# Two layer normalisations in a cross-attention and mixture-of-experts kernel: subtract and multiply replaced by multiply and add

## The chip, the cores and the metric

The kernel runs on one core of one Trainium2 chip. The metric is device time in microseconds (us) of one execution, as the median of several runs. The core has five engines that run side by side and wait for each other by semaphores: TensorE (PE in the profile, with its weight loads as PEld), VectorE (DVE), ScalarE (ACT), GpSimd (POOL) and SyncE (SP, which here only issues transfers).

## The reference

`x` holds 8 batches of 256 channels by 512 positions. Two blocks follow each other, each on a normalised input, each added to its input:

```python
def _layernorm(x, axis=-1, eps=1e-05):
    m = jnp.mean(x, axis=axis, keepdims=True)
    v = jnp.var(x, axis=axis, keepdims=True)
    return (x - m) / jnp.sqrt(v + eps)
...
x = x + _L0_xattn_ref(_layernorm(x, axis=-1), ctx_2048, mask, mask, Wq, bq, Wk, bk, Wv, bv)
x = x + _L0_ffn_ref(_layernorm(x, axis=-1), router_w, shared_gate, shared_up, shared_down, w_gate, w_up, w_down)
```

The first block is cross-attention with 16 heads of 16 channels over 512 by 512 positions; queries come from the normalised `x`, keys and values from the context. The second sees each of the 256 rows of a batch as a token of 512 features: one shared feed-forward network for all, and a router (softmax over 8 experts, the best two) that sends each token to two expert networks of 352 hidden features in bfloat16. The feed-forward block itself returns `x + shared_out + routed` with the normalised tokens as its `x`, so the sum gets the normalised tokens once more.

## The kernel before

The program is one list of instructions in an order written by hand (`tc.manual_schedule()`); each engine takes its own in that order, so an instruction that waits holds up all that stands behind it on its engine. The main loop runs over 8 batches (`b`), 4 groups of heads in each (`g`, in the code `G` counts them over all batches), and 8 steps in each group (`h`); `n = 8 * g + h` numbers the 32 steps of a batch.

In each step TensorE makes two sets of scores: one for the row maximum of a coming group (`row_max`, L453 into the PSUM buffer `s1`, of which there is one), one with the positions turned for the current group (`exp_scores`, L499). VectorE takes the maximum of the first (`nm`, L460), ScalarE the exponential of the second (`e`, L508), and TensorE multiplies it with the values (`attend`, L524). A group ends with `turn_sums` (L539) and `divide` (L554 to L556): the reciprocal of the sums, times the mask (L555), times the summed values (L556). L555 and L556 read two tensors each from the on-chip memory (SBUF).

Between these steps, at step numbers that stand in tables (`ROUTE`, `SHARED`, `FFN`, the conditions on `n`), lie the projections of the next groups (L431, `extra_rows` at L421, L438), the values of the next batch (L393), the shared network of the batch before (L117), its router (`route`, with `hit` at L659, `ranked` at L662, `only` at L668, `left` at L671, `rows` at L710, all small VectorE instructions on two SBUF tensors), and transfers. After the last batch's attention (from about 661 us on) come the expert tiles and the last batch's own feed-forward part.

The change touches the two normalisations. `norm_stats` gives for 128 rows a mean (`mv[:, 0:1]`, VectorE) and an inverse deviation (`rs`, a power on GpSimd at L354).

- The attention normalisation, `start_norm`, runs on GpSimd for batches 1 to 7: steps 9 and 11 of the batch before, one half of the channels each. L374 makes `xm` from `x`; L375 multiplies it by the mask `mb`. Between or before them stand the two L361 of `mask_context` (context times mask, step 8, in batch 0 step 10). Batch 0's own normalisation is written out elsewhere (`shifted`, `scaled`, L1211).
- The token normalisation, `token_norm`, runs once for each half of a batch's tokens: on GpSimd for batches 0 to 6, on VectorE for the last batch. L575 makes `xn`; L576 adds it to the running sum `acc`; on GpSimd the cast to bfloat16 (L604) and a memset (L605) follow for the first half, and TensorE turns `xn` (L594).

Of the kernel before, what the change touches and what calls it, by code (L numbers as in the profile page):

```python
# [9 lines left out]
F32 = mybir.dt.float32  # L10
# [3 lines left out]
ALU = mybir.AluOpType  # L14
# [3 lines left out]
P = 128  # L18
# [22 lines left out]
def xattn_ffn_kernel(  # L41
# [20 lines left out]
    nc = tc.nc  # L62
# [3 lines left out]
    def pool(name, bufs, **kw):  # L66
        return ctx.enter_context(tc.tile_pool(name=name, bufs=bufs, **kw))
# [6 lines left out]
    four = pool("four", 4)  # L74
# [280 lines left out]
        return mv, rs  # L355


    def mask_context(b, engine=nc.gpsimd):
        s = S[b]
        for i in range(2):  # L360
            engine.tensor_mul(s["ctx"][:, i, :], s["ctx"][:, i, :], s["mb"])  # L361
# [5 lines left out]
    def start_norm(b, i):  # L367

        s = S[b]
        if i == 0:  # L370
            s["xm"] = one.tile([P, 2, T], F32, tag="xm", name=f"xm{b}")
        xm = s["xm"]
        mv, rs = s["stats", i]
        nc.gpsimd.tensor_scalar(xm[:, i, :], s["x"][:, i, :], mv[:, 0:1], rs, ALU.subtract, ALU.mult)  # L374
        nc.gpsimd.tensor_mul(xm[:, i, :], xm[:, i, :], s["mb"])  # L375

    def project_v(b, sc):
# [192 lines left out]
    def token_norm(b, tt, engine=nc.gpsimd):  # L570
        s = S[b]
        acc = s["acc", tt]
        mv, rs = s.pop(("tstats", tt))
        xn = one.tile([P, T], F32, tag="rd", name="xn")
        engine.tensor_scalar(xn, acc, mv[:, 0:1], rs, ALU.subtract, ALU.mult)  # L575
        engine.tensor_add(acc, acc, xn)  # L576
        s["xn", tt] = xn

# [631 lines left out]
    busy(6)  # L1210
    nc.vector.tensor_scalar(s0["xm"][:, 1, :], s0["xm"][:, 1, :], s0["stats", 1][1], None, ALU.mult)  # L1211
    mask_context(0, nc.vector)
    q_part, q_rows = project_qk(0, 0)
    k_part, k_rows = project_qk(0, 1)
# [27 lines left out]
    for i in range(3):  # L1242
# [11 lines left out]
        out=mwide, in_=mask.rearrange("b o (n t) -> (b o n) t", t=32).rearrange("p (o t) -> p o t", o=1).to_broadcast([P, 4, 32])  # L1254
# [32 lines left out]
    def clear(i):  # L1287
# [8 lines left out]
    clears = [(1.0, lambda i=i: clear(i)) for i in range(E * PIECES)]  # L1296
    FFN = {
        0: {4: residual, 6: token_stats, 7: token_norm, 9: turn_tokens, 14: round_tokens},
        2: {6: residual, 7: token_stats, 8: token_norm, 9: turn_tokens, 10: round_tokens},
    }  # L1300
    LAST_FFN = {3: residual, 5: token_stats}
# [55 lines left out]
    for b in range(B):  # L1357
# [13 lines left out]
        if 0 < b < B - 1:  # L1371
            spread(plan, route(b - 1), ROUTE)
            units, early = shared_units(b - 1, True)
            spread(plan, units, SHARED)
            plan[28].append(early)
        elif b == B - 1:
            units, early = shared_units(b - 1, True)
            spread(plan, units[:24], SOONER)
            plan[20].append(early)
            units = units[24:]  # L1380
            first_rows = route(b - 1, rows_first=True)
            row_map, expert_numbers = expert_map(0)
            fetch, named, experts, tiles = expert_tiles()
            spread(plan, first_rows, FIRST_ROWS)
            spread(plan, row_map, ROW_MAP)
            plan[FETCH_AT] += expert_numbers + [fetch]
            plan[22] += [lambda: ring.remove(0)]
            plan[22] += [go for _, go in units[:2]]
            units = units[2:]
            plan[29] += [lambda: divide(last - 2), lambda: experts(0)]  # L1390
            plan[26] += [lambda: token_norm(b, 0, nc.vector)]
        later = plan[STEPS:]
        plan = plan[:STEPS]
        for g in range(NG):
            G = NG * b + g
            for h in range(8):
# [44 lines left out]
                if b + 1 < B:  # L1441
                    if n == (4 if b else 8):
                        load_batch(b + 1)
                    elif n == 7 and b:
                        start_stats(b + 1, 0)
                    elif n == (8 if b else 10):
                        mask_context(b + 1)
                    elif n == 9 or n == 11:
                        start_norm(b + 1, n // 11)
                    elif n in V_AT:  # L1450
                        for sc, kc in V_AT[n]:
                            if kc == 0:
                                NEWV[sc] = project_v(b + 1, sc)
                            if kc < 2:
                                NEWV[sc][0](kc)
                            else:
                                NEWV.pop(sc)[1]()
# [109 lines left out]
```

## Time and profile before

| | |
|---|---|
| median of 3 runs | 799.71 us (797.23 to 801.35) |
| the profiled execution | 799.23 us, of which the span from first to last instruction is 797.5 |
| busy, share of the span | TensorE 96%, VectorE 71%, ScalarE 43%, GpSimd 41% |
| L374, 14 on GpSimd | 2111 ns each |
| L575, 14 on GpSimd and 2 on VectorE | 2090 ns and 546 ns each |

A row of the time line reads: start in us from the span's start, duration in us, engine, line of the program, operation, the tiles it writes and reads (`out<-in`), shapes, number of instructions in the row, and in brackets how long the engine idled before it and what ended that. A row of the groups has in place of the times, behind the bar, the busy time in us of all of them, the mean of one in ns, and the idle time before them. The chain that ended last is followed back from the last instruction, at each step to what released it; its shares say which engine set the end.

### The profile page before, as it was taken

The page shows a single profiled execution, that of the slowest core. Times are in us where ns is not written, and L with a number is a line of the kernel's source. Part 1 is how long each engine was busy: PE and PEld are TensorE (multiplying, and loading weights), DVE is VectorE, ACT ScalarE, POOL GpSimd, SP SyncE. Part 2 cuts the span into 40 slices and gives each one's busy share as a digit, 9 for nine tenths or more (in the row PEclk, how much of TensorE's full clock was granted, in tenths as well). Part 3 has the DMA queues.
Part 4 walks back from the last instruction along what each step waited for, and adds up shares of the span by engine and source line. Part 5 has one row for each costly group of instructions (what it writes and reads, how often), then busy time and mean ns, then how long its engine had stood idle before and what let it go on. Part 6 is the DMA issues. An engine that isn't in the chain of part 4 may idle for free.

```text
span 797.5 us, 14542 instructions
## 1 busy us (share of the span) xinstructions
PE 764.1 (96%) x5317; PEld 315.2 (40%) x5317; DVE 566.8 (71%) x1088; ACT 346.4 (43%) x428; POOL 324.8 (41%) x451
## 2 busy tenths in 40 slices
PE   8987897999999999999999999999999999999996
PEld 5322231343333333343334333433343343665672
DVE  7676767678777877787778777888687767563315
ACT  4234444444444444443444444444444445455640
POOL 4006132804193319331843174317550234376530
PEclk9999999999999999999999999999999999999999
DMA  5115669721255325532454132210000001596739
GB/s 177 37 52 174 223 210 260 188 46 20 72 102 91 81 59 105 99 83 59 100 103 83 42 65 67 65 41 28 30 1 1 28 30 37 120 188 149 149 121 351
DMA packets 102208, 78.49 MB, mean 98 GB/s; under 512 B 69512, under 2 KB 87858, under 8 KB 101754
## 3 DMA queue, kind: packets, MB, share of 16 engines
q1 hardware_dynamic: 93674, 56.29, 26.8%
q0 software_dynamic: 5136, 20.46, 11.5%
q10 hardware_dynamic: 3328, 0.81, 0.6%
q8 instruction: 43, 0.70, 0.4%
q14 instruction: 27, 0.22, 0.1%
HBM read 38.09 MB, written 43.38 MB: 102 GB/s over the span
## 4 chain that ended last, share of the span: by engine, by line
PE 86%; DVE 11%; issue 1%; DMA 1%; ACT 0%; POOL 0%; ACTq 0%; DVEq 0%; POOLq 0%
PE s L453 33%; PE av L524 13%; DVE nm L460 8%; PE psy L117 4%; PE psk L431 4%; PE psq L431 4%; PE pg L117 4%; PE psv L117 3%; PE pu L117 3%; PE ey L947 3%; PE pgu L117 3%; PE s L499 3%; PE eg L927 3%; PE eu L927 3%; PE pht L939 1%
## 5 line engine op out<-in xcount | busy, mean ns | idle before, releaser
L508 ACT ACTIVATE e<-s 128x1024 f32<-128x1024 f32 x256 | 261.7, 1024 | 347.1 <-PE s L499 335.9
L460 DVE TENSOR_REDUCE nm<-s 128x2 f32<-128x1024 f32 x248 | 304.0, 1226 | 139.8 <-PE s L499 123.7
L453 PE MATMUL s<-k,q 32*128 32x512 f32 x1024 | 288.5, 641 | 19.1 <-DVE nm L460 17.2
L499 PE MATMUL s<-q,k 32*128 32x512 f32 x1024 | 285.5, 640 | 1.9 <-DMA q<-nmt 0.9
L524 PE MATMUL av<-e,V 128*32 128x512 f32 x1024 | 136.5, 604 | 0.0
L453 PEld LDWEIGHTS s<-k,q 32*128 32x128 f32 x1024 | 76.9, 183 | 125.0 <-DVE nm L460 115.2
L564 POOL TENSOR_TENSOR acc<-acc,x 128x512 f32<-128x512 f32 x15 | 19.0, 1268 | 186.0 <-DVE acc L563 150.3
L499 PEld LDWEIGHTS s<-q,k 32*128 32x128 f32 x1024 | 77.0, 183 | 7.4 <-ACT e L508 5.0
L354 POOL TENSOR_TENSOR rs<-ve,mhalf 128x1 f32<-128x1 f32 x32 | 18.5, 578 | 136.6 <-DVE ve L352 136.6
L421 POOL TENSOR_SCALAR extra<-mb,alpha,beta 128x512 f32<-128x512 f32 x60 | 45.9, 773 | 48.9 <-DVE q L438 22.8
L524 PEld LDWEIGHTS av<-e,V 128*32 128x32 f32 x1024 | 20.4, 108 | 97.2 <-issue 73.1
L117 PE MATMUL psy<-sdT,h 128*32 128x256 f32 (+2 forms) x336 | 54.3, 393 | 0.5 <-DVE h L1041 0.5
L933 DVE SCALAR_TENSOR_TENSOR hz<-eth,eu 128x352 bf16<-128x352 f32 x39 | 20.3, 520 | 35.1 <-PE eu L927 18.3
L209 POOL DMA_INDIRECT xs<-xnb,at x32 | 34.6, 1080 | 21.8 <-DVE at L718 11.3
L117 PEld LDWEIGHTS psy<-sdT,h 128*32 128x32 f32 (+1 forms) x336 | 29.4, 140 | 33.9 <-issue 30.6
L117 PE MATMUL pg<-xT,sguT 128*32 128x256 f32 (+1 forms) x284 | 37.0, 380 | 0.0
L117 PE MATMUL pu<-xT,sguT 128*32 128x256 f32 (+1 forms) x284 | 36.8, 382 | 0.0
L117 PE MATMUL psv<-WvT,ctx 128*128 128x256 f32 (+1 forms) x170 | 36.5, 401 | 0.0
L431 PE MATMUL psq<-xm,WqT 128*128 128x512 f32 x64 | 35.6, 641 | 0.5 <-DVE xm L1211 0.5
L117 PE MATMUL pgu<-xT,sguT 128*32 128x256 f32 (+2 forms) x234 | 35.7, 382 | 0.0
L431 PE MATMUL psk<-ctx,WkT 128*128 128x512 f32 x64 | 35.4, 640 | 0.0
L927 PEld LDWEIGHTS <-late_ctx 128*128 128x128 bf16 x312 | 29.2, 98 | 13.8 <-issue 1.3
(210 smaller groups left out, 883.4 us busy)
## 6 DMA issues: line engine op xcount, KB each, us to landing
xs<-blank SPq DMA_DIRECT2D x32, 544.0 KB
x<-in_x_dram SPq DMA_DIRECT2D x7, 512.0 KB
ctx<-in_ctx_dram SPq DMA_DIRECT2D x7, 512.0 KB
accd<-acc SPq DMA_DIRECT2D x12, 256.0 KB
again<-accd POOLq DMA_DIRECT2D x12, 256.0 KB, 3.9
out_dram<-again SPq DMA_DIRECT2D x12, 256.0 KB
gu<-in_L_ffn_w_gate_dram POOLq DMA_DIRECT2D x8, 352.0 KB, 6.2
gu<-in_L_ffn_w_up_dram POOLq DMA_DIRECT2D x8, 352.0 KB, 4.5
```

What stands on the lines that cost most here:

```text
L117: nc.tensor.matmul(ps[cols], weights[:, cols], moving, **flags)
L209: i = nc.gpsimd.indirect_dma_start(to[:, :], bass.IndirectOffsetOnAxis(ap=rows, axis=0), what, None, **bounds).ins
L421: engine.tensor_scalar(t, S[b]["mb"], at, be, ALU.mult, ALU.add)
L431: nc.tensor.matmul(ps, W[:, kc, g // 2], rhs[:, kc, :], start=(kc == 0), stop=(kc == 1),)
L453: nc.tensor.matmul(ps[:, jj, :], q[r, tci * P : (tci + 1) * P], k[r, :], start=True, stop=True)
L460: best = lambda: nc.vector.reduce_max(to, ps, axis=AX.X)
L499: nc.tensor.matmul(ps[:, jj, :], k[r, sc * P : (sc + 1) * P], q[r, :], start=True, stop=True)
L508: nc.scalar.activation(e, ps, AF.Exp)
L524: nc.tensor.matmul(AVT[G][32 * j : 32 * j + 32, :], V[:, sc, g // 2, j, g % 2 : g % 2 + 2, :].rearrange("p o d -> p (o d)"), et[j // 2][:, ...
L927: nc.tensor.matmul(ps, xT[:, kc, :], weights_of(t, GU, I, (m * NKC + kc) * I), start=(kc == 0), stop=(kc == NKC - 1),)
L933: nc.vector.scalar_tensor_tensor(HZ[t % 2], th, 1.0, pu, ALU.add, ALU.mult)
L947: nc.tensor.matmul(ps, ht[:, ic, :], weights_of(t, DN, T, ic * T), start=(ic == 0), stop=(ic == 2))
```

## The change

A new function, `normal`, makes a column `off = mean * rs * (-1)` and then `out = row * rs + off`. Both normalisations call it, on the engine they ran on before. The column is one more instruction on one element per partition, on GpSimd 28 times and on VectorE twice; the large instruction stays one, with the same shapes and two column operands, and its operations are a multiply and an add instead of a subtract and a multiply. The large instruction waits for the column by a semaphore on its own engine. `off` has four buffers. On all other engines the order of instructions stays as it was.

```diff
+    def normal(out, row, stats, engine):
+
+        mv, rs = stats
+        off = four.tile([P, 1], F32, tag="off", name="off")
+        engine.tensor_scalar(off, mv[:, 0:1], rs, -1.0, ALU.mult, ALU.mult)
+        engine.tensor_scalar(out, row, rs, off, ALU.mult, ALU.add)
+
...
         xm = s["xm"]
-        mv, rs = s["stats", i]
-        nc.gpsimd.tensor_scalar(xm[:, i, :], s["x"][:, i, :], mv[:, 0:1], rs, ALU.subtract, ALU.mult)
+        normal(xm[:, i, :], s["x"][:, i, :], s["stats", i], nc.gpsimd)
         nc.gpsimd.tensor_mul(xm[:, i, :], xm[:, i, :], s["mb"])
...
     def token_norm(b, tt, engine=nc.gpsimd):
         s = S[b]
         acc = s["acc", tt]
-        mv, rs = s.pop(("tstats", tt))
         xn = one.tile([P, T], F32, tag="rd", name="xn")
-        engine.tensor_scalar(xn, acc, mv[:, 0:1], rs, ALU.subtract, ALU.mult)
+        normal(xn, acc, s.pop(("tstats", tt)), engine)
         engine.tensor_add(acc, acc, xn)
```

## The prediction

> **What bounds the kernel now.** I read the page from the top: engines and the chain that ended last, then the GpSimd groups, then the time line of VectorE and GpSimd wherever the distance between two row maxima (`nm`, L460) was longer than usual.
>
> ```profile
> PE 764.1 (96%) x5317; PEld 315.2 (40%) x5317; DVE 566.8 (71%) x1088; ACT 346.4 (43%) x428; POOL 324.8 (41%) x451
> PE 86%; DVE 11%; issue 1%; DMA 1%; ACT 0%; POOL 0%; ACTq 0%; DVEq 0%; POOLq 0%
> ```
>
> TensorE is busy 96% of the span and GpSimd (POOL), which the change relieves, is 0% of the chain. From 60 to 661 us the kernel beats in steps of 2.45 to 2.60 us: TensorE makes scores in one PSUM buffer, VectorE takes their maximum in 1.23 us, and the next scores go 0.09 us later into the same buffer. In a batch of 32 steps TensorE idles under 1 us of 81. So a VectorE instruction that ends late in its step moves everything behind it; a GpSimd instruction matters only through VectorE.
>
> ```profile
> L421 POOL TENSOR_SCALAR extra<-mb,alpha,beta 128x512 f32<-128x512 f32 x60 | 45.9, 773 | 48.9 <-DVE q L438 22.8 <-DVE share L685 15.4 <-DVE k L438 10.2
> L374 POOL TENSOR_SCALAR xm<-x,mv,rs 128x512 f32<-128x512 f32 x14 | 29.6, 2111 | 0.0
> L575 POOL TENSOR_SCALAR xn<-acc,mv,rs 128x512 f32<-128x512 f32 x14 | 29.3, 2090 | 1.2
> L726 POOL TENSOR_SCALAR xnb<-place 128x1 int32<-128x1 f32 x32 | 7.2, 226 | 4.5 <-DMA xs<-xnb,at 2.5
> ```
>
> Behind the bar of each row stand the busy time in us, the mean of one instruction in ns, and the idle time before them. L421 is a multiply and an add with two column operands, which is what the normalisations become; L374 and L575 are a subtract and a multiply of the same shape. Next, how the engines touch each other (VectorE first, then GpSimd, the sixth of the seven attention normalisations):
>
> ```profile
> 471.35 0.17 DVE L555 TENSOR_TENSOR rd<-rd,mturn 128x16 f32<-128x16 f32 x1
> 471.55 1.38 DVE L556 TENSOR_TENSOR O<-u,rd 128x256 f32<-128x256 f32 x1
> 473.01 1.21 DVE L460 TENSOR_REDUCE nm<-s 128x2 f32<-128x1024 f32 x1
> ...
> 469.18 2.08 POOL L374 TENSOR_SCALAR xm<-x,mv,rs 128x512 f32<-128x512 f32 x1
> 471.34 1.31 POOL L375 TENSOR_TENSOR xm<-xm,mb 128x512 f32<-128x512 f32 x1
> ```
>
> L556 usually takes 0.42 us. Here it ends 0.28 us after L375 does: a VectorE instruction that reads two SBUF tensors waited for GpSimd. The step took 3.08 us instead of 2.50. Of all VectorE instructions only eight are stretched this way, by 4.5 us in all, and three of the steps are longer for it: at 62.23 us (L555 and L556 behind both L361; 4.04 us), at 469.93 and at 551.61 (3.08 each). That is 1.6 + 0.6 + 0.6 us, the most that the change could give back here.
>
> **GpSimd's own gain.** The small operation is not in the trace. One column costs 0.19 us as a copy (L727), 0.226 as one add (L726), 0.578 as a power (L354). L421's own fixed part is its 0.773 less what 511 more columns cost a cast (L604 0.622 against L727 0.187): 0.34. I take 0.28, between L726 and that; 0.20 and 0.58 stay as ends. A GpSimd instruction that waits for the one before starts 0.09 us later (L374 to L375: 471.26 to 471.34). So a normalisation takes 0.28 + 0.09 + 0.77 = 1.14 us instead of 2.09: 0.95 us less, 27 us over 28. TensorE waits for L575 in 2 places and 1.2 us in all, so none of the 27 is on the path: GpSimd waits longer for VectorE instead. What counts is that what follows each normalisation on GpSimd comes 0.95 us (behind two, 1.9 us) earlier, and which two-input VectorE instruction it then meets.
>
> **Token normalisation, six batches (starts 180.50, 261.69, 343.15, 424.69, 506.40, 588.07).** In each, L659 starts 1.23 us after L575:
>
> ```profile
> 181.73 0.17 DVE L659 TENSOR_TENSOR hit<-w,best 128x16 f32<-128x16 f32 x1
> 181.93 0.17 DVE L662 TENSOR_TENSOR hit<-hit,rank 128x16 f32<-128x16 f32 x1
> 182.67 1.23 DVE L460 TENSOR_REDUCE nm<-s 128x2 f32<-128x1024 f32 x1 [0.57 <-PE s L499]
> ...
> 180.50 2.08 POOL L575 TENSOR_SCALAR xn<-acc,mv,rs 128x512 f32<-128x512 f32 x1
> 182.66 1.28 POOL L576 TENSOR_TENSOR acc<-acc,xn 128x512 f32<-128x512 f32 x1
> ```
>
> Both lie under L575's second half and are not held. After the change: column 180.50 to 180.78, `xn` 180.87 to 181.64, L576 (two inputs, 1.27 us) ready at 181.73, just when L659 starts. At 471.34 and 471.35 such a tie went to VectorE. Then L576 runs 181.90 to 183.17, and L662, due at 181.93, ends near 183.20. The maximum, due at 182.67, starts at 183.12: 0.45 us late. 0.08 us of that is slack (it ends 0.17 us before the next scores, where 0.09 is enough). 0.37 x 6 = +2.2 us.
>
> **Attention normalisation, seven batches.** First (60.17): L375 ends at 62.67 instead of 63.62, the two L361 at 65.15 instead of 66.06, and L556 behind them 0.9 us sooner: -0.9, all on the path. Second: L375 runs 143.74 to 145.01 and holds L555 (144.86) for 0.15 us, which idle time covers. Third to fifth: the second normalisation is ready at 227.36, L556 starts at 227.34: VectorE first, 0; if GpSimd is 0.1 us earlier, L556 waits until 228.13 and the maximum is 0.4 us late: 0 to +1.2 for three. Sixth and seventh: L375 now runs 469.44 to 470.72, the second normalisation 471.09 to 471.86 holds L555 until 471.88, and L556 (471.92) ties with the second L375 (471.95). VectorE first: 0.58 better than before; GpSimd first: 0.58 worse. I take 0, bounds -1.2 to +1.2. A late L421 in the last batch meets L556 near 594.5: +0.1.
>
> [...]
>
> **The two on VectorE (672.58 and 692.7).** Each gets one more column instruction; the nearest row is L352, 0.154 us, plus 0.03 before the next. The first stands in a stretch (661 to 674) with no idle VectorE, ahead of L576 and L556: +0.2. The second has idle time around it: 0. The large instruction stays at its 0.546 us. Ends 0 and +0.4. Nothing moves on TensorE, ScalarE or SyncE; the casts and scatters on GpSimd's queue start up to 1 us earlier and nothing waits for them there.
>
> **Sum.** -0.9 + 2.2 + 0 + 0.1 + 0.2 = +1.6 us. The profiled execution took 799.23 (span 797.5 and 1.7 around it): 800.8. It lies 0.48 under the median of 799.71, so 801.3.
>
> **Rivals.** *The column is cheap, and GpSimd wins the ties (slower).* With 0.20 us L576 is ready at 181.65, 0.08 ahead of L659, as the second L361 (64.80) was ahead of L556 (64.91) and won. L659 then waits until 182.95; the cast L604 (0.62 us), which follows L576 without a gap, takes its turn before L662 as the second L361 did; L662 ends near 183.5 and the maximum is 0.78 late, 0.70 beyond slack: x 6 = 4.2. The third to fifth batch lose their 1.2. 4.2 + 1.2 - 0.9 + 0.3 = +4.8: 804.5. It decides below about 0.23 us for the column. For it: L726's 0.226. Against: two operands and two operations, as L421's fixed 0.34.
>
> *The column is dear (faster).* At L354's 0.58 us `xn` ends at 181.94; L659 and L662 pass before L576, covered by 0.57 us of idle time. The first batch gains 0.6, sixth and seventh 0.5 each, less 0.3 at the end: -1.3, so 798.4. The same comes about if 16-element instructions slip through; L555 at 63.72 took 1.16 and speaks against that.
>
> *The change does not do what it says:* the new form takes 2.09 us, and the column is added. Then GpSimd is 0.37 us later each time: the sixth and seventh batch's L556 escape L375 (-1.0), the first gains 0.8, +0.3 at the end: -1.5, 798.2. Sixty L421 at 0.773 speak against it.
>
> **Chances.** Forecast 0.42, cheap column 0.37, dear column 0.12, no effect on the form 0.09. 0.5% is 4.0 us, about what a measurement of this kernel can tell from no change (its three runs span 4.1). Slower: 0.31 of the cheap column, 0.06 of the forecast with the ties against it, 0.01 else: 0.38. Faster: 0.06, from the last two with the ties for them. Same: 0.56. The range reaches from under the last two, 797.5, to above the cheap column, 805.5.
>
> **What would show it.** Right: the normalisations on GpSimd near 0.77 us, the column near 0.28; L662 near 1.2 us in six batches with steps near 2.95; the step at 62 us near 3.2. The cheap column: L659 near 1.2 too, steps over 3.2. Wrong altogether: L659 and L662 at 0.17 and still a change beyond 4 us; or TensorE waiting on something other than the row maximum.

## The result, and the profile after

The changed kernel takes 797.51 us (median of 12 runs, 796.05 to 798.31) against 799.78 for the kernel before (12 runs, 797.23 to 802.85). The ratio is 0.9956, with a 95% interval of 0.9941 to 0.9971: some 2.3 to 4.7 us faster, where 1.6 us slower was forecast. That the median lies at the very lower end of the forecast's range (797.5) is luck: this end came from two rivals, a dear column and a form without effect, and neither of them happened. The profiled execution took 796.99 us, 795.2 of it the span.

The page of the changed kernel, engines and chain (its line numbers are 5 to 7 higher behind the new function: L453 is L459, L499 L505, L375 L381, L576 L581, L662 L667):

```profile
PE 762.2 (96%) x5317; PEld 315.2 (40%) x5317; DVE 573.4 (72%) x1090; ACT 346.4 (44%) x428; POOL 295.0 (37%) x479
PE 85%; DVE 12%; issue 1%; DMA 1%; ACT 0%; DVEq 0%; ACTq 0%
```

GpSimd lost 29.8 us of work, VectorE gained 6.6 us of occupied time, and the chain is TensorE and VectorE as before. The groups of the changed kernel on GpSimd (and, last, the column on VectorE):

```profile
L363 POOL TENSOR_SCALAR xm<-x,rs,off 128x512 f32<-128x512 f32 x14 | 11.6, 825 | 1.4
L363 POOL TENSOR_SCALAR xn<-acc,rs,off 128x512 f32<-128x512 f32 x14 | 10.7, 767 | 1.4
L362 POOL TENSOR_SCALAR off<-mv,rs 128x1 f32<-128x1 f32 x28 | 7.5, 267 | 1.2
...
L362 DVE TENSOR_SCALAR off<-mv,rs 128x1 f32<-128x1 f32 x2 | 0.4, 192 | 0.7 <-POOL rs L354 0.7
```

The prices were right: 0.767 us for the large instruction (0.825 in the attention, where some waited for VectorE), 0.267 for the column. So were most of the places named. The forecast new wait is there, in the time line of VectorE and GpSimd in the third batch:

```profile
260.69 0.16 DVE L664 TENSOR_TENSOR hit<-w,best 128x16 f32<-128x16 f32 x1
260.89 1.12 DVE L667 TENSOR_TENSOR hit<-hit,rank 128x16 f32<-128x16 f32 x1
261.94 1.21 DVE L466 TENSOR_REDUCE nm<-s 128x2 f32<-128x1024 f32 x1
...
259.82 0.77 POOL L363 TENSOR_SCALAR xn<-acc,rs,off 128x512 f32<-128x512 f32 x1
260.67 1.30 POOL L581 TENSOR_TENSOR acc<-acc,xn 128x512 f32<-128x512 f32 x1
```

L581 starts 0.02 us before L664, and yet L664 is not held (0.16 us). L667 is: it ends 0.04 us after L581, after 1.12 us instead of 0.17. The step is 2.91 us long instead of 2.60.

To see where time went I took the time from each row maximum to the next in two traces and listed the steps that differ. A second trace of before (e1, below) is the base, since single traces have stretches in which, by their clock record, TensorE was granted half its clock: the first trace of before has one from 32.4 to 35.8 us (mean granted clock 0.51, 1.1 us lost), the one of the changed kernel none until its end.

| place in the trace of the changed kernel | step before to after | change, next step included |
|---|---|---|
| 61 us, L561 free of the first L368 | 4.04 to 3.08 | -0.96 |
| 157 us, scores L505 hardly late (0.25 us) | 3.48 to 2.73 | -0.75 |
| 177 us, L664 and L667 wait | 2.60 to 3.39 | +0.66 |
| 259, 340, 422, 503, 585 us, L667 waits | 2.60 to 2.91 | +0.18 each |
| 470 and 551 us, L562 free of L381 | 3.08 to 2.50 | -0.50 each |
| all steps from 54 to 659 us | | -1.1 |

The first row on VectorE, in the first trace of before and then after: the second of the two instructions is still held, the first no longer.

```profile
63.72 1.16 DVE L555 TENSOR_TENSOR rd<-rd,mturn 128x16 f32<-128x16 f32 x1
64.91 1.44 DVE L556 TENSOR_TENSOR O<-u,rd 128x256 f32<-128x256 f32 x1
```

```profile
62.73 0.19 DVE L561 TENSOR_TENSOR rd<-rd,mturn 128x16 f32<-128x16 f32 x1
62.95 1.44 DVE L562 TENSOR_TENSOR O<-u,rd 128x256 f32<-128x256 f32 x1
```

The second row was in no term of the forecast. TensorE around it, with two weight casts of GpSimd and four small transfers of SyncE ahead of it, in the first trace of before and then after:

```profile
151.79 0.61 POOL L333 DMA_DIRECT2D d<-in_L_ffn_w_down_dram  x1
152.51 2.45 SPq L481 DMA_DIRECT2D q<-nmt  x4
153.04 0.49 POOL L333 DMA_DIRECT2D gu<-in_L_ffn_w_gate_dram  x1
...
157.41 1.13 PE L453 MATMUL s<-k,q 32*128 32x512 f32 x4
158.61 1.13 PE L499 MATMUL s<-q,k 32*128 32x512 f32 x4
```

```profile
147.02 0.60 POOL L333 DMA_DIRECT2D d<-in_L_ffn_w_down_dram  x1
148.24 0.49 POOL L333 DMA_DIRECT2D gu<-in_L_ffn_w_gate_dram  x1
150.56 3.97 SPq L487 DMA_DIRECT2D q<-nmt  x4
...
155.46 0.70 PE L459 MATMUL s<-k,q 32*128 32x512 f32 x2
155.71 0.70 PE L505 MATMUL s<-q,k 32*128 32x512 f32 x2
```

At the first scores of a later group the two kinds run side by side: in the fourth batch of the changed kernel L459 starts at 318.82 us and L505 at 318.94. Here, before, L499 starts 1.2 us after L453: the first scores of a new group wait for `q`, into which four small transfers write the row maxima (`take_max`, L481, `q<-nmt`). The casts moved from 0.7 us before and 0.5 us behind the first of these transfers to 3.5 and 2.3 us before it.

### The profile page after: what moved, and what is told of

Same layout as the page of the kernel before. It is cut to its first block, busy times and chain, and to the rows that moved or that the text cites. A ratio compares the mean times of both kernels' runs of the same rounds, so it can differ in the third digit from the quotient of the medians.

```text
span 795.2 us, 14572 instructions
## 1 busy us (share of the span) xinstructions
PE 762.2 (96%) x5317; PEld 315.2 (40%) x5317; DVE 573.4 (72%) x1090; ACT 346.4 (44%) x428; POOL 295.0 (37%) x479
## 4 chain that ended last, share of the span: by engine, by line
PE 85%; DVE 12%; issue 1%; DMA 1%; ACT 0%; DVEq 0%; ACTq 0%
PE s L459 32%; PE av L530 13%; DVE nm L466 9%; PE psy L117 4%; PE psq L437 4%; PE psk L437 4%; PE pgu L117 4%; PE pg L117 4%; PE ey L952 3%; PE psv L117 3%; PE eg L932 3%; PE eu L932 3%; PE s L505 3%; PE pu L117 2%; PE pht L944 1%
## 5 line engine op out<-in xcount | busy, mean ns | idle before, releaser
L459 PE MATMUL s<-k,q 32*128 32x512 f32 x1024 | 287.8, 639 | 19.0 <-DVE nm L466 16.5
L505 PE MATMUL s<-q,k 32*128 32x512 f32 x1024 | 285.0, 639 | 1.8 <-DMA q<-nmt 0.8
L459 PEld LDWEIGHTS s<-k,q 32*128 32x128 f32 x1024 | 76.7, 183 | 124.8 <-DVE nm L466 115.9
L505 PEld LDWEIGHTS s<-q,k 32*128 32x128 f32 x1024 | 76.8, 183 | 6.2 <-ACT e L514 4.9
```

The costliest lines, as they stand in the source:

```text
L459: nc.tensor.matmul(ps[:, jj, :], q[r, tci * P : (tci + 1) * P], k[r, :], start=True, stop=True)
L505: nc.tensor.matmul(ps[:, jj, :], k[r, sc * P : (sc + 1) * P], q[r, :], start=True, stop=True)
```

## The experiments

Theory A (in the expectations the VectorE or place theory): the gain is what VectorE waits less for GpSimd, plus chance. Theory B (the transfer theory): besides, GpSimd's queue, 2 to 3 us ahead after several shorter normalisations, starts its weight casts (L333, 352 KB each) earlier, and the small transfers into `q` are no longer slowed by them. Theory C (the clock theory): the change raises the granted clock.

Each kernel ran in 8 to 12 runs beside 19 to 35 of before on the same chip. Because the times go with the mean granted clock (before, beside e5: 799.45 us at 0.997, 806.31 at 0.99), the table also gives the time at a granted clock of 0.998, from a straight line fitted with one slope to all runs that were taken together (0.58 to 0.65 us per 0.001; standard error of a value 0.25 to 0.4 us).

| run | ratio to before (95%) | at equal clock, against before |
|---|---|---|
| e1 before again | 1.0002 (0.9980 to 1.0024) | 800.4, 800.0 |
| e2 attention only | 0.9948 (0.9928 to 0.9967) | 798.0, 800.0 |
| e3 token only | 1.0002 (0.9982 to 1.0022) | 800.3, 800.0 |
| e4 before, cast early | 0.9987 (0.9966 to 1.0009) | 799.6, 800.0 |
| e5 after again | 0.9966 (0.9949 to 0.9982) | 798.6, 799.8 |
| e6 after, pause | 0.9963 (0.9945 to 0.9982) | 796.7, 799.8 |
| e7 after, cast late | 1.0007 (0.9993 to 1.0021) | 801.5, 799.8 |
| e8 after, old work too | 1.0019 (0.9999 to 1.0039) | 802.0, 799.8 |
| e9 after, two pauses | 0.9935 (0.9908 to 0.9961) | 796.1, 800.0 |
| e10 after, third time | 0.9957 (0.9938 to 0.9975) | 798.2, 800.0 |
| e11 = e6 again | 0.9957 (0.9941 to 0.9973) | 795.7, 798.4 |
| e12 = e8 again | 1.0014 (0.9993 to 1.0034) | 800.4, 798.4 |

**e1, before again** (no edit).

> The kernel before, unchanged, for a second trace. Two theories of where the gain came from. VectorE theory: only what GpSimd holds VectorE up for has changed (L555 and L556 at about 62, 472 and 553 us; new waits of L662 in six batches), and the rest of the difference between the two traces (a stretch at half clock from 32.4 to 35.8 us in the one of before, late scores L499 at about 158, 321 and 403 us) is chance: then these last are not there again in this trace, and the steps at 62, 470 and 552 us are long as before (4.04, 3.08, 3.08). Transfer theory: the late scores at about 158, 321 and 403 us belong to the kernel before, because its casts L333 start just ahead of the small transfers from nmt into q; then L499 is late by 0.35 to 1.2 us there again. Time: same as before within 0.2% by both.

The steps at 61 (4.04), 468 and 550 us (3.08) came back to the hundredth, and so did the late scores in the second batch (L499 0.99 us late, step 3.48). Those near 321 and 403 us did not. So the first belongs to the kernel, the other two come and go.

**e2, the attention normalisation alone; e3, the token normalisation alone.**

```diff
 e2: start_norm calls normal(...); token_norm keeps
+        engine.tensor_scalar(xn, acc, mv[:, 0:1], rs, ALU.subtract, ALU.mult)
 e3: token_norm calls normal(...); start_norm keeps
+        nc.gpsimd.tensor_scalar(xm[:, i, :], s["x"][:, i, :], mv[:, 0:1], rs, ALU.subtract, ALU.mult)
```

> Only the attention normalisation (L374) is a multiply and an add; the token normalisation is as before. VectorE theory: -0.96 at 62 us, -0.5 each at 472 and 553 us, no new wait of L662: about 2.0 us faster than before, so 0.3 to 1 us faster than the whole change. Transfer theory adds what the earlier casts bring: GpSimd's queue is 2 us ahead after two normalisations instead of 3 to 4, the casts L333 lie 1 to 2 us further from the small transfers, and the late scores at 158, 321 and 403 us shrink or vanish: 2 to 3.5 us faster than before.

> Only the token normalisation (L575) is a multiply and an add. VectorE theory: L662 waits in six batches (+0.18 to +0.37 each), the step at 62 us stays at 4.04, and the chain on GpSimd ahead of L375 is 1 us earlier in six batches, so that L375 lies from 470.4 to 471.7 and L555 waits for it a little: time within 0.15% of before, by -1 to +1.5 us. Transfer theory: the casts come 1 us earlier, and the late scores at 158, 321 and 403 us are there but shorter: -1.5 to +1.

The attention half holds all of the gain. In e2 the steps at 64, 470 and 552 us shrink by 0.95, 0.5 and 0.5, scores are at most 0.25 us late, nothing waits in the router; but in the second to fifth batch a new wait of 0.2 to 0.4 us appears (steps of 2.83 to 2.96), because with one shorter normalisation instead of two GpSimd meets the divide in another place. e3 has its six new waits (+0.18 each), late scores still at 162 and 325 us (0.5 us each, as theory B expects of casts that come only 1 us earlier), the same new waits at the divide, and yet the steps at 470 and 552 us are short as well: one shift of 1 us is enough to take L381's counterpart away from the divide. Its time is that of before. All this was expected in kind, but e3's gain at 470 and e2's new waits had not been seen ahead.

**e4, before with the cast of step 11 at step 7.**

```diff
-                plan[5 * n + 1].append(casts.pop(0))
+                plan[(1, 6, 7, 16, 21, 26)[n]].append(casts.pop(0))
```

> The kernel before with one edit: in batches 1 to 4 the cast that stood at step 11 (L333, d<-w_down) stands at step 7, ahead of the attention normalisation in GpSimd's queue. The normalisations are as before. VectorE theory: nothing that GpSimd holds VectorE up for changes, the time is that of before. Transfer theory: the transfers from nmt into q (step 13) no longer share the DMA engines with that cast, the late scores at 321 and 403 us go, and at 158 us, where two casts stood around, half of it: 0.6 to 1.6 us faster than before.

The step near 161 us went from 3.48 to 3.03, half, as theory B has it for one of two casts. In the later batches e1 had no late scores that could go. The time, 0.13% less, cannot be told from none; the fall that theory B expected was 0.6 to 1.6 us.

**e5, after again.**

> The changed kernel again, beside runs of before on the same chip. The first four runs showed two parts: steps that differ in the traces (about -1.0 us for the whole change against a second trace of before, counted place by place), and stretches at half clock, of 3.4 us each, which come at different places in each run and cost some 0.6 us per 0.001 of mean granted clock. Place theory: the change is worth 1 to 2 us, and what the medians show beyond that is chance of the clock; then the mean granted clock of its runs is that of the runs of before within 0.001. Clock theory: less work on GpSimd lets the clock be granted more often; then its mean clock is again over that of before by 0.002 or more, and the time lower by 2.5 to 4 us. In the trace both expect no late scores L505 after 60 us, the long steps at about 177 (3.39) and four or five of 2.91.

The same steps as in the first trace, place by place; the count gives -1.3 us against e1, and at equal clock it is 1.2 us faster than before. Its mean granted clock is 0.0023 over that of before, which is what the clock theory expected.

**e7, after with that cast one step later; e8 and e12, after with the old work added.**

```diff
 e7
-                plan[5 * n + 1].append(casts.pop(0))
+                plan[(1, 6, 12, 16, 21, 26)[n]].append(casts.pop(0))
 e8, e12, in start_norm behind the mask multiply
+        mv, rs = s["stats", i]
+        nc.gpsimd.tensor_scalar(spare, s["x"][:, i, :], mv[:, 0:1], rs, ALU.subtract, ALU.mult)
```

> The changed kernel with the cast of step 11 (L333, d<-w_down, batches 1 to 4) at step 12, behind one scatter in GpSimd's queue, so that in batches 2 to 4 it starts about 1 us before the small transfers from nmt into q, as in the kernel before. Transfer theory: late scores come back in batches 2 to 4 (0.2 to 0.5 us each, at about 238, 319, 400 us), not in batch 1, where the queue has no scatter at that place: +0.3 to +1.2 us over the changed kernel. If the late scores have another cause: no late scores and the same time.

> The changed kernel, and behind each mask multiply of the attention normalisation GpSimd also does the old subtract and multiply (2.1 us, 14 times) into a tile that nobody reads (bfloat16, for room). GpSimd is as busy as before and its queue is 2 us later after each half. Clock theory: the mean granted clock falls to that of before (about 0.993 to 0.995). Place theory: the clock stays with that of the changed kernel; only places move: the casts L333 start later again, so the step near 157 us is long again (3.0 to 3.6 instead of 2.73), and L562 at 62 us escapes one of the two context multiplies: within 1.5 us of the changed kernel.

At equal clock e7 is 3.0 us slower than the changed kernel and 1.8 slower than before, by the start of three casts. Theory B had the places right and the size wrong (0.3 to 1.2 us). GpSimd, SyncE and TensorE of e7 in the fourth batch:

```profile
317.77 0.58 POOL L333 DMA_DIRECT2D d<-in_L_ffn_w_down_dram  x1
...
318.53 3.35 SPq L487 DMA_DIRECT2D q<-nmt  x4
...
323.43 1.13 PE L459 MATMUL s<-k,q 32*128 32x512 f32 x4
325.12 1.13 PE L505 MATMUL s<-q,k 32*128 32x512 f32 x4 [0.56 <-ACT logT L1061]
```

The cast starts 0.76 us ahead of the four transfers. Issuing them takes 3.35 us instead of 2.2, and L505 is 1.69 us late (the step takes 4.18 us). The profile puts the wait down to ScalarE's `logT`, which L505 does not read and which in the changed kernel's own trace runs after L505 has begun (`logT` from 319.79 to 320.16 us, L505 from 318.94); what L505 does read is `q`. The transfer records of the traces show it. For the 64 packets of 128 bytes that such a group of four moves, the table gives when the last packet ends and when the last semaphore of the four reports its landing, both counted from the start of the first issue:

| kernel, batch | cast starts before the transfers by | last packet after | landed after | scores late by |
|---|---|---|---|---|
| all, no cast near | | 2.96 to 3.22 us | up to 3.6 us | mostly 0.12 us |
| after, third to fifth | 3.6 us | 3.00 to 3.02 | 3.57 to 3.63 | 0.12 |
| after, second (two casts) | 3.5 and 2.3 | 4.71 | 5.01 | 0.25 |
| before, third | 1.0 | 3.66 | 3.98 | 0.12 |
| e1, third to fifth | 1.0 | 3.64 to 3.94 | 4.06 to 4.62 | 0.15 to 0.20 |
| before, fourth and fifth | 1.0 | 4.27, 4.26 | 5.10, 5.23 | 0.40, 0.46 |
| before, second (two casts) | 0.7, and 0.5 behind | 5.20 | 5.96 | 1.19 |
| e7, third | 0.7 | 6.03 | 6.86 | 2.09 |
| e7, fourth and fifth | 0.8 | 4.99, 4.56 | 6.39, 5.33 | 1.69, 0.56 |

The scores are due 4.9 us after the first issue. Where the landing came within 4.62 us they were at most 0.26 us late (before, after, e1); where it came after 5.01 us or more, they started 0.13 to 0.20 us behind it, in every trace. So the landing is what they wait for. In the changed kernel's second batch the transfers are still slowed (last packet after 4.71 us), but land after 5.01 us, 0.1 behind the due time. Where the transfers lose the time is not separated: issuing them takes longer too, up to 3.97 us instead of 2.24. Part of it is in the packets. In the second batch of before, 16 packets of a cast (22.5 KB and about 2 us each) start from 153.10 to 153.71 us, and the first of them to end does so at 155.46; the first small packet, which with no cast near starts 1.2 us after the first issue (175.15 against 173.98), starts 3.0 us after it, at 155.51. That fits the shared DMA engines of e4's expectation; the records name a packet's queue, not its engine.

e8 shows the same from the other side: with GpSimd as far behind as before, its casts start 0.1 us before to 0.3 us behind the transfers, and four batches have late scores (0.7 to 2.3 us). At equal clock it is 3.5 us slower than the changed kernel, where the place theory expected at most 1.5. That two causes, the extra work and the lateness, are in e8 together is why e7 is the cleaner case: it has the same work as the changed kernel.

**e6 and e11, after with a pause before the add.**

```diff
         normal(xn, acc, s.pop(("tstats", tt)), engine)
+        if tt == 0 and 0 < b < B - 1:
+            engine.memset(pause, 0.0)
         engine.tensor_add(acc, acc, xn)
```

> The changed kernel with one more instruction: in batches 1 to 6 a memset of 128 x 512 bfloat16 (write only, about 0.5 us) on GpSimd between the first token normalisation and the add that follows it, so that L664 and L667 pass before the add reads SBUF. If those waits cost what the place count says (0.66 at 177 us, 0.18 in each of five batches, 1.5 us in all), the six long steps go back to about 2.6, L667 to 0.17 us, and the time is 1.0 to 1.6 us under the changed kernel's, unless the clock differs. If they are hidden: same time as the changed kernel.

GpSimd now writes for 0.53 us, without reading a tensor, while the two router instructions pass. VectorE, then GpSimd, of e6:

```profile
259.65 0.17 DVE L667 TENSOR_TENSOR hit<-w,best 128x16 f32<-128x16 f32 x1
259.85 0.17 DVE L670 TENSOR_TENSOR hit<-hit,rank 128x16 f32<-128x16 f32 x1
260.59 1.23 DVE L467 TENSOR_REDUCE nm<-s 128x2 f32<-128x1024 f32 x1 [0.57 <-PE s L506]
...
258.79 0.77 POOL L364 TENSOR_SCALAR xn<-acc,rs,off 128x512 f32<-128x512 f32 x1
259.49 0.53 POOL L583 MEMSET pause<- 128x512 bf16 x1
259.99 1.26 POOL L584 TENSOR_TENSOR acc<-acc,xn 128x512 f32<-128x512 f32 x1
```

All six long steps are gone, and the count against e1 is -3.0 us where e5 has -1.3. The medians of e5 and e6 do not show it (799.31 and 799.36), since e6's runs happened to have a clock 0.0024 lower; at equal clock e6 is 1.9 us under e5.

**e9, e6 and a second pause; e10, after beside it.**

```diff
                     elif n == (8 if b else 10):
+                        for _ in range(0 if b else 4):
+                            nc.gpsimd.memset(pause, 0.0)
                         mask_context(b + 1)
```

> The changed kernel with the pause before the add of the token normalisation (as in e6) and four such write-only memsets (about 2.1 us) on GpSimd ahead of the two context multiplies L368 in batch 0, so that the divide of that time (two SBUF inputs) passes before them. By the place count the step at 61 us goes from 3.1 to about 2.5 (-0.6) on top of the 1.5 us of e6: 2.1 us under the changed kernel, 3 us under before at the same clock. If it is hidden or only moves: the step at 61 us or the next one is longer by the same 0.6.

> The changed kernel once more beside e9 on the same chip, to compare the two there: e9 is 1 to 2.5 us faster than this, with their mean granted clocks taken into account. Its own mean clock against that of before says again whether the clock goes with the change (0.002 or more above) or with chance.

The step at 62 us is 2.45, as long as its neighbours, where the first trace of before had 4.04. e9 is the fastest kernel here, ratio 0.9935 against 0.9957 for the changed kernel beside it, 2.1 us at equal clock.

**e11 and e12, for the clock.**

> The kernel of e6 again, for the clock. So far the kernels without the old attention form (e2, e5, e7, e9, e10) had a mean granted clock 0.0015 to 0.0034 over that of before in the same call, those with it (e1, e3, e4, e8) -0.0003 to +0.0005, and e6, without it, -0.0001. If the old form's work on GpSimd is what costs clock, this run comes out 0.0015 or more above before, and the time at 0.995 of it; if the clock is chance, anything from -0.002 to +0.003.

> The kernel of e8 again, in which GpSimd also does the old subtract and multiply, for the clock. If that work costs clock: its mean clock is within 0.0008 of that of before and 0.0015 or more below e11's. If the clock is chance: no such order. The late scores near 158, 241, 324 and 409 us come back by the transfer theory, and the time is 2 us or more above the changed kernel's.

The mean granted clock against before was +0.0023 and +0.0034 for the changed kernel (e5, e10), +0.0022 for e2, but -0.0001 and +0.0015 for one and the same kernel (e6, e11), and +0.0006 and +0.0018 for the other (e8, e12), +0.0015 for e7, +0.0021 for e9 and within 0.0004 of it for e1, e3 and e4, mostly with a standard error near 0.0008. That the old form's work costs clock is not borne out: e12 has that work and the higher clock. Theory B held in e12: late scores in the same four batches, and at equal clock 2.0 us slower than before.

## Why the prediction was wrong, point by point

- **GpSimd's own gain: right.** Column 0.28, measured 0.267; form 0.77, measured 0.767; none of it on the path directly.
- **Token normalisation, +2.2 forecast, +1.6 measured.** Mechanism and place were right in five of the six batches; a wait there costs 0.18 and not 0.37, because the step is 0.31 longer and the next gives 0.13 back. At 177 us GpSimd won the tie (L581 at 178.79, L664 at 178.83), and it cost 0.66, close to the 0.70 that the cheap column rival gave; in e5 and e12 it went the same way, in e7, e8 and e10 VectorE won, so it is a matter of hundredths (GpSimd 0.04 us ahead here, 0.02 us ahead at 260.67, where L664 was not held).
- **First attention normalisation, -0.9 forecast, -0.96 measured;** third to fifth 0 and 0 (L562 went first and the normalisation was the one stretched, to 1.01 to 1.05 us). The late L421 forecast near 594.5 (+0.1) did not show.
- **Sixth and seventh: 0 taken, -0.5 each measured.** The tie went to VectorE as at 471.35 in the trace of before. VectorE first, then GpSimd, in the changed kernel:

```profile
469.01 0.48 DVE L561 TENSOR_TENSOR rd<-rd,mturn 128x16 f32<-128x16 f32 x1
469.53 0.43 DVE L562 TENSOR_TENSOR O<-u,rd 128x256 f32<-128x256 f32 x1
...
468.71 0.77 POOL L363 TENSOR_SCALAR xm<-x,rs,off 128x512 f32<-128x512 f32 x1
469.56 1.52 POOL L381 TENSOR_TENSOR xm<-xm,mb 128x512 f32<-128x512 f32 x1
```

  L561 waits for the second normalisation, L562 follows 0.03 us before L381, and L381 is the one that is stretched (1.52 instead of 1.27). The same reasoning that was used for the token ties would have given VectorE here; taking the middle cost 1.0 us.
- **The step that failed: "the casts and scatters on GpSimd's queue start up to 1 us earlier and nothing waits for them there".** They start 2.6 to 2.8 us earlier against the transfers (3.6 us ahead instead of 1.0), as several normalisations stand before them, and the transfers into `q`, which TensorE waits for, land earlier (in the second batch 5.01 us after their first issue instead of 5.96). The forecast put this at nothing without looking at the transfers. It was worth -0.75 to -0.87 us in the second batch in the traces of the changed kernel, and up to 0.35 more at each of two other places in one of the two traces of before. The late L499 at 158, 321 and 403 us stood in the trace of before as steps of 3.68, 2.88 and 2.95, and the forecast passed over them with "the most that the change could give back here", counting only steps with a held VectorE instruction.
- **The two on VectorE:** 0.192 us each, near 0.18. Whether the first cost 0.2 at the end is not settled: the part from the last row maximum on took 136.3 to 141.5 us in the traces, with half-clock stretches in it and a wait of TensorE for `hT` near 715 us, which was 0.36 us in one trace of before and 2.21 in the other.
- **The sum** with the measured terms of e5: -0.96 + 1.56 - 1.0 - 0.87 = -1.3 us, which is its count and its time at equal clock (-1.2). So of the 2.9 us between forecast and count the sixth and seventh normalisation make 1.0, the transfers 0.87, the size of the token waits 0.64, and the small terms the rest. Each moved the forecast the same way; the transfers alone would not have turned its sign.
- **What stays open:** the medians show 2.3 to 4.7 us. What goes beyond 1.2 to 1.9 us goes with the mean granted clock, which was 0.0023 and 0.0034 higher for the changed kernel on the two chips on which the clocks of both kernels are listed (e5, e10); e11 and e12 did not settle whether that is chance. The clock records of the 14 traces have 21 stretches at half clock ahead of the last microseconds, and every one of them starts during an idle time of TensorE of 0.78 us or more, or within 3 us behind it; most such idle times have none. The wait in the long step at 62 us is one of these places. In the four kernels that keep it at 2.3 us (before, e1, e3, e4) two of the traces have a stretch right behind it; in the ten others, with 0.7 to 1.4 us, none has. TensorE behind this wait, in before (0.70 us) and in e4 (1.22 us):

```profile
67.54 0.70 PE L453 MATMUL s<-k,q 32*128 32x512 f32 x2 [2.31 <-DVE nm L460]
```

```profile
67.50 1.22 PE L453 MATMUL s<-k,q 32*128 32x512 f32 x2 [2.31 <-DVE nm L460]
```

  Three more stretches stand behind late scores (e7, e8, e12). Whether shorter waits of TensorE raise the clock, so that some of the gain beyond 1.9 us would be the change's own, is the author's guess from these counts: no run tests it, and one and the same kernel differed by 0.0016 between e6 and e11.

## What to carry to other kernels

When an engine off the path gets faster, list everything that stands behind it in its queue, transfers included, with the new start of each, and look for whom it then meets: here the engine's 30 us were worth nothing, and the encounters of its queue were worth plus and minus one microsecond each. List every long step of the trace of before first and name its cause, also the ones that seem to have nothing to do with the change. Six write-only instructions of half a microsecond at the right place were worth 1.9 us, as much as the whole change at equal clock.

## What the runs showed of the hardware that was not expected

- In the trace of before, the old form (subtract and multiply, 2.07 us in these rows) held a two-input VectorE instruction for its first 0.80 us only. VectorE, then GpSimd, in the third batch:

```profile
227.13 0.18 DVE L555 TENSOR_TENSOR rd<-rd,mturn 128x16 f32<-128x16 f32 x1
229.35 0.33 DVE L710 TENSOR_TENSOR part<-hit,row 128x32 f32<-128x32 f32 x1
...
225.46 2.07 POOL L374 TENSOR_SCALAR xm<-x,mv,rs 128x512 f32<-128x512 f32 x1
228.88 2.07 POOL L374 TENSOR_SCALAR xm<-x,mv,rs 128x512 f32<-128x512 f32 x1
```

  L710, begun 0.47 us into the second L374, took 0.33 us instead of its median of 0.19 and ended 0.80 us behind that one's start (0.80 and 0.81 in the fourth and fifth batch); L555, begun 1.67 us into the first, was not held (0.18 us). The new form (0.77 us) held L561 to its end: begun 0.31 us into the L363 at 468.71, L561 took 0.48 us and ended 0.02 us behind it; at 550.39 it took 0.47 us. So in these rows each held VectorE for about 0.8 us, though one is nearly three times as long.
- The last packet of four transfers of 2 KB ended after 2.96 to 3.23 us with no cast near (before, after), after 3.64 to 6.03 when a cast of 352 KB started 0.7 to 1.0 us ahead, in one of these groups with a second cast 0.5 us behind (before, e1, e7), and after 3.00 to 3.02 when one cast started 3.6 us ahead (after); with two casts 3.5 and 2.3 us ahead it was 4.71 (after).
- In the clock records of the 14 traces, the 21 stretches at half clock ahead of the last microseconds were 3.4 us long (three of them 6.8), none to four in an execution; the one in before cost 1.1 us. Each stood in or behind an idle time of TensorE of 0.78 to 3.9 us: the one in before begins at 32.4 us, 2.0 us after an idle time of 0.78 us ahead of L499. Four of 3.4 us would make 4.4 us at the cost of that one, an estimate, or 0.55% of the time; a difference under that between two single traces is not readable before they are taken out.
